# A float32 graph network with Strassen-Winograd products by adj: the first product reads the right half of adj first, and the products that end layers 2 and 3 take adj's tiles as weights

## The chip, the core and the metric

The kernel runs on one core of one Trainium2 chip. The metric is device time in microseconds of one execution, the median over several; lower is better. The profiled execution is a run of its own, whose time is given beside its span.

## What is computed

Four layers on x (8 graphs in a batch, 2048 nodes, 64 features), all with the same 2048 x 2048 matrix adj, all float32. Each layer adds its result to x and normalizes over the features.

```python
# layer 0: A_stack = [I, adj, 2 adj adj - I]; w and b depend on the node
x = layernorm(x + einsum('bnki,nkio->bno', A_stack x, w(embedding)) + b(embedding))
# layer 1: two times z = relu((adj z) W_i)
x = layernorm(x + relu((adj relu((adj x) W_0)) W_1))
# layer 2
x = layernorm(x + x W_self + (adj x) W_neighbor + bias)
# layer 3: x_stack = [x, adj x, 2 adj(adj x) - x] for each of two equal supports
x = layernorm(x + concat(x_stack) W + bias)
```

So there are seven products of adj (2048 x 2048) with a 2048 x 512 matrix (8 graphs x 64 features). The kernel centers weights so that a mean need not be subtracted in most norms, and orders the linear maps so that layer 2 and layer 3 end with a product by adj that is added to something ready: in layer 2, slot 1 of `xy` holds x W_self + bias and slot 0 holds x W_neighbor; in layer 3, slot 1 holds x times its own weights + bias and slot 0 the rest; in both, slot 1 += adj * slot 0, and slot 1 is normalized.

## The kernel before

**Data.** `xy` holds nodes on partitions: 16 tiles of 128 nodes, two slots, 512 columns (4 pairs p of two graphs, 128 columns each). adj comes from memory in two layouts: *slices* for the first product, *blocks* for the six others. Every chunk or block of it is 1 MB and goes through a ring of buffers `a` (four at first; three more, `ring2`, from the second product's end).

**Products by Strassen-Winograd on two levels.** The outer level cuts adj into quadrants A11, A12, A22 and the sums S1 to S4, which makes seven `inner` products; each `inner` does the same once more with eight `mul`s (matrices 0 to 7, of which several are sums). The sums of adj's blocks are made once, during the first product, and kept in DRAM (`comb[q]`); the other six products load them.

**The first product (slices 0 to 3, `plain_slice` and `fast_slice`).** A slice `ns` is a quarter of the target nodes: every fourth tile. It needs four chunks, chunk j holding source nodes of quarter j; chunks 0 and 1 are adj's left half, 2 and 3 its right. The loads are asked for on SP's queue (`slice_chunk`, L149). While TensorE multiplies, VectorE forms the sums (`prepare`, L473): `outer` makes S1 to S4, `inner` makes the second-level sums of each. POOL's queue writes them out (L485, `comb<-si` and `comb<-so`; four buffers `si`, three `so`). Slice 0 is multiplied plainly, chunk by chunk in the order 0, 1, 2, 3 (L618, 128 records of 512 columns). Slices 1 to 3 use the seven outer products (L655) in this order: A11, A12, S1, S2, A22, S3, S4, with T1 to T4, sums of x, against them. `prepare` is a generator and `next(parts)` runs it piece by piece between these products. Results go into `hT` (features on partitions), to DRAM (`t1T`), and by transposes (`back`, L339) into slot 1 of `xy`. `join_bias` adds layer 0's bias to x in the last slice; `sum_weights` and `sum_wn` prepare weights of later layers on VectorE in slices 1 and 2.

**The six other products (`product`).** The order of the outer products is A11, S1, A12, S2, S4, S3, A22. A `mul` is

```python
for m in range(TG):
    nc.tensor.matmul(ps, xb[:, m, :], a[:, :, m, :], ...)   # L228
```

that is, 128 x 128 pieces of x (or a sum of x) are the weights, 512 columns of adj stream past, and the result has features on partitions. A float32 matmul shows as two records in the trace, so a `mul` has eight. VectorE combines the banks (`add`, L201). `onto` adds to what is there: `early` adds the terms that are ready, `finish` the last one, and `hand_over` gives a finished block to the `Pump`, a list of generators that `pump.step` advances once or more per `mul`. The jobs are the features of a layer (`feature1a`, `feature3`, ..., with `project`, L840) and the norms (`layernorm`, L355 to L384).

In the products that end layers 2 and 3 the job is `onto_rest`: it transposes a finished block back to nodes on partitions, four transposes (L889), and adds it to slot 1 (L890). Then the norm follows, and in layer 3 the store.

**Order.** Each engine runs its instructions in the order fixed when the program was built: a scheduler places them by priorities that follow the program's order, and instructions marked `tc.keep_in_program_order` (also called `pin` here) stay in that order among themselves.

Of the kernel before, what the change touches and what calls it, by code (L numbers as in the profile page):

```python
# [9 lines left out]
F32 = mybir.dt.float32  # L10
# [6 lines left out]
P = 128  # L17
# [78 lines left out]
def kernel(  # L96
# [53 lines left out]
        return a  # L150

    chunks = {}
    chunks[0, 0] = slice_chunk(0, 0, TG)
    for t in range(TG):
        nc.scalar.dma_start(xy[:, t, 0, :], x[:, t, :])
    for j in range(1, NG):
        tq = slice(j * TG, (j + 1) * TG)
        nc.sync.dma_start(xy[:, tq, 0, :], x[:, tq, :])
        chunks[0, j] = slice_chunk(0, j)
# [12 lines left out]
    def xcol(slot, t, p):  # L172
        return xy[:, t, slot, ts(p, 2 * F)]


    loads = 0
    banks = 0
# [11 lines left out]
            nc.sync.dma_start(a, comb[q][s].rearrange("p (n m c) -> p n m c", n=TG, m=TG))  # L189
        return a  # L190

    def product(src, feature, between=None, rate=1, own=None, pin=False, batch=1):

# [4 lines left out]
        def add(out, a, b, op=ALU.add):  # L200
            nc.vector.tensor_tensor(out, a, b, op)  # L201
            return out
# [7 lines left out]
        def inner(q, b, finish, early=None):  # L210
# [13 lines left out]

            def mul(ps, s, xb, start, stop=True):
                a = load(q, s)
                for m in range(TG):
                    nc.tensor.matmul(  # L228
                        ps, xb[:, m, :], a[:, :, m, :], start=(start and m == 0),
                        stop=(m == TG - 1), skip_group_check=True,  # L230
                    )
                pump.step(pump.rate)
# [39 lines left out]
        def onto(c, base, give=None, then=None):  # L272

            def early(blk, plus):
                add(c[:, blk, :], base[:, blk, :], plus)

            def finish(blk, ps, plus):
                add(c[:, blk, :], ps, (base if plus is None else c)[:, blk, :])
                if give is not None:
                    hand_over(c, *give, blk)  # L280
                if then is not None:
                    then(blk)
            return finish, early

        def hand_over(c, ih, ch, blk):
            pump.add(feature(2 * ih + blk // 2, 2 * ch + blk % 2, c[:, blk, :]))
# [40 lines left out]

        def last(blk):
            add(v[:, blk], v[:, blk], u[:, blk])
            hand_over(v, 1, 1, blk)  # L330

        inner(S3, t3, *onto(u, u, then=last))
# [75 lines left out]
    if True:  # L408
# [30 lines left out]
            center(wn.rearrange("p n d o -> p (n d) o"), pin=pin)  # L439

        def sum_weights(w3):

            for k in range(2):
                half = slice(k * F, (k + 1) * F)
                nc.vector.tensor_tensor(wd[half, W3A, half], w3[half, 1], w3[half, 3], ALU.add)
                nc.vector.tensor_tensor(w3[half, 2], w3[half, 2], w3[half, 4], ALU.add)
                nc.vector.tensor_tensor(wd[half, W3X, half], w3[half, 0], w3[half, 2], ALU.subtract)
                nc.vector.tensor_scalar(wd[half, W3AA, half], w3[half, 2], 2.0, None, ALU.mult)


            for k in range(2):
                half = slice(k * F, (k + 1) * F)
                center(wd[half, W2N:, half], half)
            for w in (W2S, W3X):
                nc.vector.tensor_tensor(wd[:, w, :], wd[:, w, :], ident, ALU.add)
            for k in range(2):
                half = slice(k * F, (k + 1) * F)
                for n, w in enumerate((W3A, W3X)):
                    nc.vector.tensor_copy(w3o[half, n], wd[half, w, half])
                for n, w in enumerate((W2N, W2S)):  # L460
                    nc.vector.tensor_copy(w2o[half, n], wd[half, w, half])
            center(b2.unsqueeze(1))
            center(b3.unsqueeze(1))

# [1 line left out]
        def prepare(ns, ch, outers):  # L468
# [42 lines left out]
            def put(q, s):  # L511
# [2 lines left out]
                keep(q, 3, flat[:, 3:])  # L514
                inner(q, *(flat[:, k].rearrange("p (m n) -> p m n", m=TG) for k in range(4)))

            outers[S1] = s1 = outer(rq(1, 0), rq(1, 1), ALU.add)
            outers[S2] = s2 = outer(sq(s1), rq(0, 0), ALU.subtract)
            inner(A11, *raw(0, 0))
            outers[S3] = s3 = outer(rq(0, 0), rq(1, 0), ALU.subtract)  # L520
            yield
            put(S1, s1)
            yield
            put(S2, s2)
            outers[S4] = s4 = outer(rq(0, 1), sq(s2), ALU.subtract)
            inner(A12, *raw(0, 1))
            inner(A22, *raw(1, 1))
            yield
            put(S3, s3)
            put(S4, s4)  # L530
# [2 lines left out]
        with tc.tile_pool(name="p_n", bufs=4, space=PSUM) as p_n, tc.tile_pool(  # L533
# [28 lines left out]
            def xq(h, c):  # L562
# [3 lines left out]


            T = [
                xy[:, 2:NT:TG, 1, :].rearrange("p t (h c) -> p t h c", h=2),
                xs.tile([P, NT // 4, 2, 4 * F], F32, tag="T2", name="T2"),  # L570
                xy[:, 3:NT:TG, 1, :].rearrange("p t (h c) -> p t h c", h=2),
                xs.tile([P, NT // 4, 2, 4 * F], F32, tag="T4", name="T4"),
            ]

            def sums_of_x():
# [33 lines left out]
            def plain_slice(ns, ch):  # L609

                ps = [bank() for p in range(NP)]
                for j in range(NG):
                    steps = [(p, m) for p in range(NP) for m in range(TG)]
                    if j == 0:

                        steps = [(p, m) for m in range(TG) for p in range(NP)]
                    for k, (p, m) in enumerate(steps):
                        mm = nc.tensor.matmul(  # L618
                            ps[p],
                            xcol(0, TG * j + m, p),  # L620
                            ch[j][:, m],
                            start=(j == 0 and m == 0),
                            stop=(j == NG - 1 and m == TG - 1),
                            skip_group_check=True,
                        )
                        if j == k == 0:
                            tc.keep_in_program_order(mm)
                hT = [new_h() for p in range(NP)]
                for p in range(NP):
                    nc.scalar.copy(hT[p], ps[p])  # L630
                return hT

            def fast_slice(ns, ch, held):
# [44 lines left out]
                    return u  # L678

                next(parts)  # L680
                pa = mul(bank(), raw(0, 0), x_of(0, 0))
                p1 = sums.tile([P, GW], F32, tag="p1", name="p1")
                nc.scalar.copy(p1, pa)
                load_chunks(ns + 1, 0, 1)
                next(parts)
                p2 = mul(bank(), raw(0, 1), x_of(1, 0))
                if ns == TG - 1:
                    join_bias(0, 1)
                    join_bias(0, 0)
                pc = mul(bank(), summed(S1), t_of(1))  # L690
                for job in held:
                    pump.add(back(*job))
                next(parts)
                if ns == 1:
                    sum_weights(w3)
                elif ns == 2:
                    sum_wn()
                pb_ = mul(bank(), summed(S2), t_of(2))
                u2 = plus("u2", pb_, p1)
                done(0, p2, p1)  # L700
                pd = mul(bank(), raw(1, 1), t_of(4))
                load_chunks(ns + 1, 2, 3)
                nc.vector.tensor_tensor(u2, pc, u2, ALU.add)
                next(parts)
                if ns == TG - 1:
                    join_bias(1, 0)
                mul(pb_, summed(S3), t_of(3), start=False)
                u3 = plus("u3", pb_, p1)
                done(3, pc, u3)
                done(2, pd, u3)  # L710
                pe = mul(bank(), summed(S4), x_of(1, 1))
                done(1, pe, u2)
                return [hT[p] for p in range(NP)]

            for ns in range(TG):
                ch = [chunks.pop((ns, j)) for j in range(NG)]
                if ns == 0:
                    for n, _ in enumerate(prepare(ns, ch, {})):
                        if n == 1:
                            sums_of_x()  # L720
                    hT = plain_slice(ns, ch)
                    w3 = load_weights()
                    load_chunks(1, *range(NG))
                    pump.add(biases())
                else:
                    hT = fast_slice(ns, ch, held)
# [116 lines left out]
                )  # L843
        return z

    def part(g, p, slot):
        return xy[:, g * TG : (g + 1) * TG, slot, ts(p, 2 * F)]


    def feature1a(g, p, hT):  # L850
        nc.scalar.activation(part(g, p, 1), project([(hT, W1A)]), AF.Relu)
# [30 lines left out]
            yield  # L882
        return own

    def onto_rest(g, p, hT):

        pt = p_z.tile([P, TG, P], F32, tag="z", name="pt3")
        for k in range(TG):
            nc.tensor.transpose(pt[:, k, :], hT[:, ts(k, P)], ident)  # L889
        nc.vector.tensor_tensor(part(g, p, 1), pt, part(g, p, 1), ALU.add)  # L890
        yield


    product(1, then(feature1b, 0, mean=True, after=both_terms(0, w2o, b2)), rate=2)
    product(0, then(onto_rest, 1))


    def feature3(g, p, hT):
# [1 line left out]
        yield  # L900

    product(1, feature3, own=both_terms(1, w3o, b3), rate=1.5)
    product(0, then(onto_rest, 1, single=[(1, 0)], store=True), rate=2)
    pump.drain()


# [45 lines left out]
```

## Time and profile before

| what | value |
|---|---|
| median of 3 runs | 1690.9 us (1686.34 to 1692.46) |
| profiled execution, its own time | 1690.62 us |
| its span | 1688.8 us |
| PE busy | 1666.1 us, 5952 records |
| PEld (weight loads) busy | 856.5 us |
| VectorE busy | 942.0 us |
| ScalarE, POOL busy | 265.3 us, 249.6 us |
| mean granted TensorE clock | 0.996 |
| DMA | 391.25 MB, mean 232 GB/s |

The first product lies from about 5.7 to 221 us, layer 0's second product to about 770 us, layer 1's first from there, and so on; the product that ends layer 2 lies from some 1100 to 1300 us, the one that ends layer 3 in the last 200 us. In the timeline a row is a run of like instructions: start, length, engine, line, operation, output and inputs, count, and in brackets the idle time before it with what ended it. Records of matmuls overlap (a 512-column record is 593 ns long, but the next begins after some 429), so the distance of two starts is the time that a matmul takes of TensorE, not its length.

### The profile page before, as it was taken

To read this page: it belongs to the slowest core of one execution; us is meant where nothing else is said; L and a number is where in the kernel's file an instruction comes from. 1 tells how busy PE (TensorE), PEld (TensorE's weight loads), DVE (VectorE), ACT (ScalarE), POOL (GpSimd) and SP (SyncE) were. 2 spreads that over 40 slices of the span, in tenths; PEclk is the share of its full clock that TensorE was granted. 3 is DMA by queue.
4 is the path that set the end of the run, shared out by engine and by line. 5 is a ranking of instruction groups with operands and counts; after the bars stand their busy time and mean duration, and the time that the engine had idled before them with its cause. 6 is when DMAs were issued, how large, how long until landed. Compare 5 with 4: busy or idle time off the path is not lost.

```text
span 1688.8 us, 16180 instructions
## 1 busy us (share of the span) xinstructions
PE 1666.1 (99%) x5952; PEld 856.5 (51%) x5952; DVE 942.0 (56%) x1687; ACT 265.3 (16%) x763; POOL 249.6 (15%) x332
## 2 busy tenths in 40 slices
PE   9899999999999999999999999999999999999997
PEld 4588854444444444444455455554444455554443
DVE  5477884546456656454443365863557444543556
ACT  0000000332323332330011010220001011100001
POOL 1122200443344544450000000000000000000000
PEclk9999999999999999999999999999999999999999
DMA  9898978134333123309877877667888866678883
GB/s 326 328 353 329 331 275 303 62 123 166 109 114 123 52 86 125 112 19 376 303 268 264 310 253 257 226 216 283 291 296 282 306 210 237 231 265 309 316 310 121
DMA packets 82271, 391.25 MB, mean 232 GB/s; under 512 B 8880, under 2 KB 25264, under 8 KB 42640
## 3 DMA queue, kind: packets, MB, share of 16 engines
q1 hardware_dynamic: 69504, 346.78, 58.4%
q0 software_dynamic: 11248, 42.08, 6.5%
q10 hardware_dynamic: 1440, 1.35, 0.2%
q8 instruction: 48, 0.79, 0.2%
q14 instruction: 31, 0.25, 0.0%
HBM read 339.85 MB, written 50.33 MB: 231 GB/s over the span
## 4 chain that ended last, share of the span: by engine, by line
PE 95%; DVE 3%; DMA 1%; POOL 0%; ACT 0%; issue 0%; POOLq 0%; DVEq 0%
PE mmb L228 25%; PE y L792 20%; PE mmc L228 17%; PE mma L228 16%; PE ps_n L655 8%; PE ps_n L618 3%; PE z L840 2%; PE z L872 2%; DMA a<-in_slices 1%; PE pt L831 1%; PE pt L889 1%; DVE ss L371 0%; PE pt_n L339 0%; DVE xy L381 0%; DVE sm L355 0%; DVE xy L356 0%
## 5 line engine op out<-in xcount | busy, mean ns | idle before, releaser
L228 PE MATMUL mmb<-a,t 128*128 128x512 f32 x1008 | 454.9, 593 | 1.1 <-DVE xy L381 1.1
L228 PEld LDWEIGHTS mmb<-a,t 128*128 128x128 f32 x1008 | 188.7, 190 | 229.0 <-issue 224.7
L800 DVE SCALAR_TENSOR_TENSOR xy<-y,e_sb,xy 128x128 f32<-128x128 f32 x512 | 179.7, 351 | 137.5 <-PE y L792 121.6
L809 POOL TENSOR_TENSOR s<-s 128x512 f32<-128x512 f32 (+2 forms) x192 | 159.0, 828 | 339.5 <-ACT s L804 329.3
L804 ACT ACTIVATE s<-y,e_sb 128x128 f32<-128x128 f32 x512 | 138.9, 382 | 270.5 <-PE y L792 270.4
L228 PE MATMUL mma<-a,T 128*128 128x512 f32 x384 | 173.3, 594 | 0.0
L201 DVE TENSOR_TENSOR u<-mmb,p 128x512 f32<-128x512 f32 x84 | 58.0, 690 | 193.8 <-PE mmb L228 188.4
L228 PE MATMUL mmc<-a,t 128*128 128x512 f32 x336 | 151.7, 594 | 0.0
L792 PE MATMUL y<-wn,xT 64*128 64x512 f32 x512 | 133.1, 592 | 0.0
L228 PE MATMUL mma<-a,xy 128*128 128x512 f32 x288 | 130.4, 594 | 2.7 <-DVE C L201 2.6
L792 PE MATMUL y<-wn,tT 64*128 64x512 f32 x512 | 131.3, 589 | 0.0
L792 PE MATMUL y<-wn,C 64*128 64x512 f32 x512 | 131.2, 589 | 0.0
L228 PEld LDWEIGHTS mma<-a,T 128*128 128x128 f32 x384 | 71.4, 190 | 84.3 <-issue 83.5
L201 DVE TENSOR_TENSOR C<-mmc,C 128x512 f32<-128x512 f32 x60 | 41.4, 690 | 101.7 <-PE mmc L228 101.7
L228 PEld LDWEIGHTS mmc<-a,t 128*128 128x128 f32 x336 | 61.9, 190 | 70.9 <-issue 70.4
L228 PEld LDWEIGHTS mma<-a,xy 128*128 128x128 f32 x288 | 53.8, 190 | 68.6 <-issue 62.9
L228 PE MATMUL mmc<-a,T 128*128 128x512 f32 x192 | 86.4, 593 | 0.0
L243 ACT COPY p<-mma 128x512 f32<-128x512 f32 x42 | 24.5, 584 | 377.8 <-PE mma L228 375.8
L792 PEld LDWEIGHTS y<-wn,xT 64*128 64x128 f32 x512 | 49.2, 187 | 63.3 <-issue 62.9
L792 PEld LDWEIGHTS y<-wn,tT 64*128 64x128 f32 x512 | 49.5, 187 | 60.6 <-issue 60.6
L792 PEld LDWEIGHTS y<-wn,C 64*128 64x128 f32 x512 | 49.6, 187 | 60.3 <-issue 60.3
L228 PE MATMUL mmc<-a,xy 128*128 128x512 f32 x144 | 64.9, 593 | 0.0
(114 smaller groups left out, 1587.9 us busy)
## 6 DMA issues: line engine op xcount, KB each, us to landing
a<-comb SPq DMA_DIRECT2D x240, 1024.0 KB, 4.8
a<-in_blocks SPq DMA_DIRECT2D x54, 1024.0 KB, 4.9
comb<-si POOLq DMA_DIRECT2D x28, 1024.0 KB, 10.9
a<-in_slices SPq DMA_DIRECT2D x15, 1024.0 KB, 8.2
comb<-so POOLq DMA_DIRECT2D x16, 512.0 KB, 5.7
comb<-so POOLq DMA_DIRECT2D x16, 256.0 KB, 5.6
t1T<-hT SPq DMA_DIRECT2D x16, 256.0 KB, 4.6
xT<-in_xT SPq DMA_DIRECT2D x16, 256.0 KB, 3.1
```

Source lines behind the costliest of these rows:

```text
L201: nc.vector.tensor_tensor(out, a, b, op)
L228: nc.tensor.matmul(ps, xb[:, m, :], a[:, :, m, :], start=(start and m == 0), stop=(m == TG - 1), skip_group_check=True,)
L243: nc.scalar.copy(p1, pa)
L618: mm = nc.tensor.matmul(ps[p], xcol(0, TG * j + m, p), ch[j][:, m], start=(j == 0 and m == 0), stop=(j == NG - 1 and m == TG - 1), skip_gr ...
L655: nc.tensor.matmul(ps[:, ts(p, GW // 2)], b(k, p), a(k // TG, k % TG), start=(start and p == k == 0), stop=(k == NT // 2 - 1), skip_group_ ...
L792: nc.tensor.matmul(y[:, b, :], terms[n][half, ts(k, P)], wn[half, n, h * DH : (h + 1) * DH, :], start=(n == 0), stop=(n == 2),)
L800: nc.vector.scalar_tensor_tensor(acc, y[:, :, ts(d, F)], e, acc, ALU.mult, ALU.add)
L804: nc.scalar.activation(s[:, d], y[:, :, ts(d, F)], AF.Copy, scale=e)
L809: nc.gpsimd.tensor_tensor(s[:, :n], s[:, :n], s[:, n : 2 * n], ALU.add)
L831: nc.tensor.transpose(pt[:, ts(k, P)], xy[:, g * TG + k, slot, ts(p, 2 * F)], ident)
L840: nc.tensor.matmul(z[:, k, :], aT[:, ts(k, P)], wd[:, w, :], start=(n == 0), stop=(n == len(terms) - 1),)
L872: nc.tensor.matmul(z[n][:, k], xT[half, ts(k, P)], w[half], start=True, stop=True)
```

## The change

Three parts, in one diff.

1. *Right half first.* Slice 0 loads and multiplies its chunks in the order 2, 3, 0, 1 (`AHEAD`). `fast_slice` takes A12 and A22 first, then A11, S1, S2, S4, S3. `prepare` forms A12's and A22's sums first, then S1, S2, S4; A11's and S3's come later. Chunks 2 and 3 of the next slice are asked for after A22, chunks 0 and 1 after S1. T1 and T4 change places. The final sums of a slice are regrouped to fit (`q3`, and `p1` with S1's product added).
2. *adj's tiles as weights.* `product` has a new argument `onto_slot`, used in the products that end layers 2 and 3. With it a `mul` is sixteen matmuls: a 128 x 128 tile of adj is the weight, 128 columns of x (or a sum of x) stream past, and the result has nodes on partitions. `early`, `finish` and `last` add slot 1 of `xy` in and write the result there. `onto_rest` with its transposes and its add is gone; the job `nothing` leads straight to the norm.
3. `sum_weights` and the centering in it are pinned to the program's order.

```diff
+    AHEAD = (2, 3, 0, 1)
+    chunks[0, AHEAD[0]] = slice_chunk(0, AHEAD[0], TG)
+    for t in range(AHEAD[0] * TG, AHEAD[0] * TG + TG):
         nc.scalar.dma_start(xy[:, t, 0, :], x[:, t, :])
-    for j in range(1, NG):
+    for j in AHEAD[1:]:
...
             def mul(ps, s, xb, start, stop=True):
                 a = load(q, s)
+                if onto_slot is not None:
+                    for k in range(TG):
+                        for m in range(TG):
+                            nc.tensor.matmul(
+                                ps[:, ts(k, P)], a[:, k, m, :], xb[:, m, :],
+                                start=(start and k == m == 0), stop=(m == TG - 1), skip_group_check=True,
+                            )
+                    pump.step(pump.rate)
+                    return
...
             def early(blk, plus):
                 add(c[:, blk, :], base[:, blk, :], plus)
+                if give is not None and onto_slot is not None:
+                    add(tiled(c[:, blk, :]), place(*give, blk), tiled(c[:, blk, :]))
 
             def finish(blk, ps, plus):
-                add(c[:, blk, :], ps, (base if plus is None else c)[:, blk, :])
+                if give is not None and onto_slot is not None:
+                    if plus is None:
+                        add(place(*give, blk), place(*give, blk), tiled(base[:, blk, :]))
+                    add(place(*give, blk), tiled(ps), place(*give, blk) if plus is None else tiled(c[:, blk, :]))
+                else:
+                    add(c[:, blk, :], ps, (base if plus is None else c)[:, blk, :])
...
         def last(blk):
             add(v[:, blk], v[:, blk], u[:, blk])
+            if onto_slot is not None:
+                add(place(1, 1, blk), place(1, 1, blk), tiled(v[:, blk]))
             hand_over(v, 1, 1, blk)
...
+            inner(A12, *raw(0, 1))
+            inner(A22, *raw(1, 1))
             outers[S1] = s1 = outer(rq(1, 0), rq(1, 1), ALU.add)
             outers[S2] = s2 = outer(sq(s1), rq(0, 0), ALU.subtract)
-            inner(A11, *raw(0, 0))
-            outers[S3] = s3 = outer(rq(0, 0), rq(1, 0), ALU.subtract)
+            outers[S4] = s4 = outer(rq(0, 1), sq(s2), ALU.subtract)
             yield
             put(S1, s1)
             yield
             put(S2, s2)
-            outers[S4] = s4 = outer(rq(0, 1), sq(s2), ALU.subtract)
-            inner(A12, *raw(0, 1))
-            inner(A22, *raw(1, 1))
+            inner(A11, *raw(0, 0))
+            yield
+            outers[S3] = s3 = outer(rq(0, 0), rq(1, 0), ALU.subtract)
             yield
             put(S3, s3)
             put(S4, s4)
...
                 next(parts)
+                p2 = mul(bank(), raw(0, 1), x_of(1, 0))
+                pd = mul(bank(), raw(1, 1), t_of(4))
+                load_chunks(ns + 1, 2, 3)
+                for job in held:
+                    pump.add(back(*job))
+                next(parts)
                 pa = mul(bank(), raw(0, 0), x_of(0, 0))
                 p1 = sums.tile([P, GW], F32, tag="p1", name="p1")
                 nc.scalar.copy(p1, pa)
+                q3 = plus("u3", pd, p1)
+                done(0, p2, p1)
...
                 pc = mul(bank(), summed(S1), t_of(1))
                 next(parts)
+                load_chunks(ns + 1, 0, 1)
...
                 pb_ = mul(bank(), summed(S2), t_of(2))
                 u2 = plus("u2", pb_, p1)
                 nc.vector.tensor_tensor(u2, pc, u2, ALU.add)
+                nc.vector.tensor_tensor(p1, pc, p1, ALU.add)
                 next(parts)
+                pe = mul(bank(), summed(S4), x_of(1, 1))
+                done(1, pe, u2)
                 if ns == TG - 1:
                     join_bias(1, 0)
                 mul(pb_, summed(S3), t_of(3), start=False)
-                u3 = plus("u3", pb_, p1)
-                done(3, pc, u3)
-                done(2, pd, u3)
-                pe = mul(bank(), summed(S4), x_of(1, 1))
-                done(1, pe, u2)
+                done(3, pb_, p1)
+                done(2, pb_, q3)
...
-    def onto_rest(g, p, hT):
-        pt = p_z.tile([P, TG, P], F32, tag="z", name="pt3")
-        for k in range(TG):
-            nc.tensor.transpose(pt[:, k, :], hT[:, ts(k, P)], ident)
-        nc.vector.tensor_tensor(part(g, p, 1), pt, part(g, p, 1), ALU.add)
-        yield
+    def nothing(g, p, c):
+        yield from ()
...
-    product(0, then(onto_rest, 1))
+    product(0, then(nothing, 1), onto_slot=1)
...
-    product(0, then(onto_rest, 1, single=[(1, 0)], store=True), rate=2)
+    product(0, then(nothing, 1, single=[(1, 0)], store=True), rate=2, onto_slot=1)
```

## The prediction

> **What bounds the kernel now.** I read the page first: engines, then the chain.
>
> ```profile
> PE 1666.1 (99%) x5952; PEld 856.5 (51%) x5952; DVE 942.0 (56%) x1687; ACT 265.3 (16%) x763; POOL 249.6 (15%) x332
> ...
> PE 95%; DVE 3%; DMA 1%; POOL 0%; ACT 0%; issue 0%; POOLq 0%; DVEq 0%
> ```
>
> TensorE is busy for all but 22.7 us, and the chain lies on it. So the change is worth what it does to TensorE's stream, to its few waits, and to the tail behind the last product. PE's waits come next:
>
> ```profile
> PE ps_n L655 <- DMA a<-in_slices: 5.5, 1, 5.5
> PE mma L228 <- DVE C L201: 2.6, 1, 2.6
> PE rise L541 <- POOL ident masks.py:199: 2.1, 1, 2.1
> ```
>
> Only the first lies where the change works (the second is at 403 us, among L792's matmuls). The timeline of PE around it:
>
> ```profile
> 70.23 1.89 PE L655 MATMUL ps_n<-a,xy 128*128 128x256 f32 x8
> 77.59 3.69 PE L655 MATMUL ps_n<-a,xy 128*128 128x256 f32 x8 [5.47 <-DMA a<-in_slices]
> 81.12 0.60 PE L339 MATMUL pt_n<-ident,hT 128*128 128x128 f32 x4
> ```
>
> SP's queue in the timeline, and the table of stages (after the stage's length: PE, PEld, DVE, ACT, POOL busy, then PEclk, DMA share, GB/s):
>
> ```profile
> 60.95 0.33 SPq L149 DMA_DIRECT2D a<-in_slices  x1
> ```
>
> ```profile
> 75.00:80.00 5.00, 2.40 (x6) 1.96 (x7) 3.20 (x6) 0.00 (x0) 0.84 (x2) 0.50 0.13 46
> ```
>
> The fourth chunk of slice 1 can be asked for only when slice 0 has read its fourth chunk (60.95), and lands 16.6 us later; slice 1 wants it at 72.1. After the wait eight records take 3.53 us (77.59 to 81.12) where eight elsewhere take 1.73: the granted clock is 0.50. The stall costs 5.5 + 1.8 = 7.3 us.
>
> Then the stages of layers 2 and 3. One `mul` is eight records (a float32 matmul is two) of 512 columns. Starts in the timeline give true pitches; durations overlap.
>
> ```profile
> 843.02 1.05 PE L840 MATMUL z<-wd,C 128*128 128x128 f32 x8
> 843.91 3.60 PE L228 MATMUL mmc<-a,t 128*128 128x512 f32 x8
> ...
> 1182.60 0.60 PE L889 MATMUL pt<-ident,C 128*128 128x128 f32 x4
> 1183.04 3.60 PE L228 MATMUL mmc<-a,t 128*128 128x512 f32 x8
> ```
>
> ```profile
> 843.02 0.86 PEld L840 LDWEIGHTS z<-wd,C 128*128 128x128 f32 x7 [0.24 <-issue]
> ```
>
> A `mul` alone is 3.434 us (from 1165.43 to 1182.60 there are five). Eight records of 128 columns, each with a fresh 128x128 weight, take 0.89 us; inside such a burst loads follow each other every (0.86 - 0.19)/6 = 0.1117 us. Four transposes take 0.44 (0.437 over several, 109.2 ns each).
>
> **The change part by part.**
>
> *Tiles of adj as weights (two of six products).* 2 x 7 x 8 = 112 calls of `mul` go from 8 records of 512 columns to 32 of 128, the shape of L840's burst: 32 x 111.7 ns = 3.574 us against 3.434, +0.140, x112 = **+15.7 us**. Bounds: below, 109.2 ns, the transposes' pitch (+6.8 us); above, 50.4 us / 384 = 131 ns, L840's busy weight-load time per record (+86 us). I take 111.7: same operands, same shape, and constant from the second record of a burst on.
>
> Here a rule speaks against the change. The Trainium skill, "TensorE: Matmul & The Clock Gate", section "Back-to-back issue gap", says that in a stream of load-and-multiply pairs the weight load sets the pace at small widths: at 128 columns about 81 ns where the formula for the multiply alone gives about 56. Those 25 ns on top of 109.2 would make 134 ns a record, 3584 x 22.5 ns = +81 us over my value, and the change clearly slower. The row shows 2.5 ns on top instead, so I follow the row; that its bursts are only eight long is what stays open.
>
> More PE instructions must also be fetched. The page's DMA queues show it:
>
> ```profile
> q8 instruction: 48, 0.79, 0.2%
> ```
>
> 48 packets for PE's 11904 instructions (one in 250; 66 bytes each), so 112 x 48 = 5376 more are 21 more packets. In the trace's DMA records two of them lie 17.7 us apart (1380.8 and 1398.5 us) with no gap at PE; the new rate is one in 14. Cost nothing; with that cover gone it is part of the third rival.
>
> *The transposes of `onto_rest` go.* 128 in all; 30 groups of four lie in the stream: 30 x 0.437 = **-13.1 us**. The last two are in the tail.
>
> *DVE.* Per product 16 adds of L890 (683 ns) go, and 16 come (three in `early` and one in `finish` for each of three inner products, four in `last`). Nothing on balance. PE waits for DVE where a bank is added to again: the read of `u2`, `u3` has one `mul`, 3.57 us, before the bank is needed. In the new order the worst case I walked (end of S3, start of A22: a final add, a whole layernorm and three adds ahead of `u2`) reads it 7.8 us after S3's end; the bank is wanted at 10.7. Cost nothing, 2.9 us of cover.
>
> *Tail.* Before, the last product stops streaming at 1673.90 + 3.43 = 1677.33, and the span ends 11.5 us later: two blocks' transposes, adds and norms interleave there. From an add (L890 at 1674.27) to the end of its norm (L381, 1677.65 + 0.69) is 4.1 us; from the last L381's end (1685.34) to the span's end 3.5. DVE takes the new chains strictly one after another, each waiting at its final add with nothing else behind it: block 3 starts 0.2 after its product, at -6.9 from the end of the stream, and ends at -2.9; block 2 ends at 1.1, block 1 at 5.2; with 3.5 that is 8.7. **-2.8 us**.
>
> *The first product.* Slice 0 now reads chunks 2, 3, 0, 1; SP's queue holds the same instructions in the same order, with other chunks in them. The last chunk asked for at 60.95 is now (1,1). Ahead of it PE does A12 and A22 (2 x 6.91), the biases (1.93), three transposed groups (1.31) and half of A11's first half (1.73): wanted at 79.5, against 77.6 before. So the stall goes, **-7.3 us**, if nothing delays the chunk. What could: the writes to `comb` on POOL's queue. A12 and A22 of slice 1 (1 MB each) are now computed before that chunk lands; `si` has four buffers, so no more than 4 MB are ever queued, but the queue stays full longer. In the DMA view of 58 to 80 us all engines move some 410 GB/s until 72; 2 MB more are at worst 5.1 us, at best nothing. I take 77.6 + 2.6 = 80.2: **+0.7 us** of wait.
>
> What else is moved. A11's sums and their write go behind S2: in slice 3 written at about 193 instead of 178.85, landed by 205; SP's load of it stands in its queue ahead of two more `a` loads and xT's, and PE wants it at 221. Ten us of cover. S1's sums are wanted at 85 instead of 79, computed 1.2 us after the chunk. `sum_weights`, now pinned behind S3's sums at about 94, is some 5.5 us of DVE; behind it `u2` (S2's product ends at 99) and so PE's S3 at 106: 6 us of cover. The chunks of slices 2 and 3 are asked for no later than before against a start 5 us earlier, and were all there (no wait in the list). T1 and T4 swap their places, nothing else. The bias joins fill DVE waits. One more 0.69 us add per slice lies in such a wait too.
>
> At the end of slice 3 a wait is *added*. Before, the last product was S4 with two short adds behind it, for columns that are transposed last. Now it is S3, with four adds (0.34 apart), and the first transposes' second halves need the third and fourth: 0.2 + 2 x 0.34 + 0.42, then one more 0.34; less the 0.44 of first halves that PE has: **+1.0 us**. DVE's next sums (t2 at about 220.4) come before PE wants them (221).
>
> **Sum:** -7.3 + 0.7 + 1.0 + 15.7 - 13.1 - 2.8 = **-5.8 us** on the profiled execution's own 1690.62 (span 1688.8 and 1.8 around it), 0.3 below the median of 1690.9: **1684.8**. A measurement of this kernel tells about 0.5% (8.5 us) from no change, so this is "within".
>
> **The rivals.**
>
> 1. *The chunk stays late.* The full 5.1 us: landing 82.7, a wait of 3.2 and perhaps part of the 1.8 for the clock: -3.3 to -1.5 us, 1687.3 to 1689.1. For it: DMA is full from 43 to 72. Against: the queue bound of 4 MB.
> 2. *Weight loads hide wholly.* At 109.2 ns per record the products pay 6.8 instead of 15.7: 1675.9, faster. For it: transposes show it. Against: their loads are shorter (141 ns against 190 in the groups).
> 3. *Weight loads become the bound.* In runs of 1800 records without a wide matmul between, the load path falls behind. Place: each product's 56 `mul`s; price 3.6 us per ns; from 113.3 ns a loss, from 115.7 slower by over 0.5%; at 131, 3584 x 19.6 ns = +69 - 5.8, 1755. For it: the page's rule, and PEld is without a gap in the bursts. Against: a burst's pitch does not grow.
> 4. *The form does not change.* The compiled order of the new kernel shows sixteen 128x128 matmuls per `mul` and no L889; nothing left for this.
>
> **How the numbers follow.** Forecast 0.62; rival 1 0.17; rival 2 0.11; rival 3 0.08; 0.02 is for things not seen. The forecast's own spread is some 4 us (0.5 ns of pitch is 1.8, the landing 2, the tail 1), so a third of it falls below 1682.4. Faster: 0.2 + 0.11 + 0.02 = 0.33; slower: 0.08 and the upper end of rival 1, 0.11; within: 0.56. The range takes in rival 1 whole and half of the way to rival 2, and leaves out rival 3: 1677.5 to 1691.5.
>
> **What would show it.** Right: L237's records 111 to 112 ns apart in both products, 3.57 us a `mul`; no PE wait on in_slices over 2 us and PEclk 1.00 at 75 to 80; 1 us of wait on hT near 213; 8 to 9 us from the last product to the end. Wrong: a pitch of 109 or over 113; a wait of several us near 79; new waits of L237 on DVE.

## The result and the profile after

The changed kernel takes 1682.19 us in the median of six runs (1681.9 to 1684.56), the kernel before 1690.7 (1686.34 to 1692.46, six runs beside them). The ratio is 0.9953, with a 95% interval of 0.9939 to 0.9966: 8.5 us less by the medians, 7.9 by the ratio. The prediction said 1684.8, 5.8 us less. The profiled execution is the slowest of the six: 1684.56, span 1682.8.

From the page after, engines, then the chain, then the packets of PE's instruction fetches:

```profile
PE 1666.6 (99%) x8176; PEld 1045.7 (62%) x8176; DVE 946.1 (56%) x1690; ACT 265.9 (16%) x763; POOL 250.3 (15%) x332
...
q8 instruction: 65, 1.06, 0.2%
...
PE 96%; DVE 3%; POOL 0%; ACT 0%; issue 0%; POOLq 0%; DVEq 0%; ACTq 0%
```

TensorE still carries the chain. DMA's 1% in it, the wait for the chunk, is gone. There are 2224 more records, and weight loads rose from 51% to 62% of the span. PE's waits (us in total, times, longest):

```profile
PE mma L244 <- DVE C L207: 2.2, 1, 2.2
PE rise L575 <- POOL ident masks.py:199: 2.1, 1, 2.1
PE pt L868 <- DVE xy L412: 1.5, 2, 1.1
PE mmb L244 <- DVE xy L412: 1.2, 1, 1.2
PE pt_n L370 <- DVE hT L704: 0.7, 1, 0.7
```

No wait on `in_slices` is left; the last row is the new wait at the end of slice 3. The third row has grown: before, its line (L831 there) was

```profile
PE pt L831 <- DVE xy L381: 1.1, 2, 0.7
```

The longer of its two waits, at 1122 us in the product that ends layer 2, is 1.08 us in the changed kernel and in e1 and e8 (part 2 alone), and 0.68 in before and in e2 (without part 2): part 2 adds 0.4 us there.

In the timeline and the table of stages, where before there were 5.47 us of idle time and a clock of 0.50:

```profile
71.40 3.62 PE L689 MATMUL ps_n<-a,xy 128*128 128x256 f32 x16
74.85 0.60 PE L370 MATMUL pt_n<-ident,hT 128*128 128x128 f32 x4
75.29 3.62 PE L689 MATMUL ps_n<-a,xy 128*128 128x256 f32 x16
78.75 0.60 PE L370 MATMUL pt_n<-ident,hT 128*128 128x128 f32 x4
...
82.64 0.60 PE L370 MATMUL pt_n<-ident,hT 128*128 128x128 f32 x4
```

```profile
75.00:80.00 5.00, 5.00 (x29) 4.46 (x27) 0.94 (x1) 1.17 (x2) 0.00 (x0) 1.00 0.58 207
```

The chunk still takes as long to land. It is asked for at 62.12 (SP's queue), and the longest "DMA to landing" of L149 is 16.9 us, so it lands at 79.0. A11's half begins at 79.18 and reads it after eight records (1.73 us), at 80.9: 1.9 us to spare. That is not much: over the seven profiles with this order of products the chunk took from 16.5 to 18.9 us, and in the slowest of them (gap=5 of e9, landing at 80.08) TensorE read it at 80.12, some 0.2 us late.

The new `mul` in the timeline, and the tail:

```profile
1663.40 3.74 PE L237 MATMUL mmc<-t,a 128*128 128x128 f32 x32
...
1666.97 3.74 PE L237 MATMUL mmb<-t,a 128*128 128x128 f32 x32
...
1670.55 3.74 PE L237 MATMUL mmc<-T,a 128*128 128x128 f32 x32
...
1674.62 0.69 DVE L412 TENSOR_TENSOR xy<-xy,rs 128x512 f32<-128x512 f32 x1
1675.23 0.68 DVE L207 TENSOR_TENSOR xy<-mmc,C 128x512 f32<-128x512 f32 x1
...
1678.62 0.69 DVE L412 TENSOR_TENSOR xy<-xy,rs 128x512 f32<-128x512 f32 x1
```

A `mul` every 3.575 us (1670.55 - 1663.40, halved). The last one stops streaming at 1670.55 + 3.57 = 1674.12, and the span ends 8.7 us later; it was 11.5. The last block's norm follows on the norm of the block before it: add at 1675.23, end at 1679.31, then the store.

The time parts cleanly at the products' starts in the traces. Six products follow the first; the fourth of them ends layer 2 and the sixth layer 3, and these two are changed by part 2. The table gives the start of the first of the six (the start of its first `mul`), the start of the fourth, and the time from there to the end of the span, in us:

| kernel, one profile each | wait for the chunk | the six products start | the fourth starts | from there to the end |
|---|---|---|---|---|
| before | 5.5 | 221.69 | 1112.81 | 576.0 |
| before, again (e7) | 5.0 | 222.38 | 1115.13 | 576.0 |
| changed | none | 216.31 | 1108.67 | 574.1 |
| part 2 alone (e1) | 2.0 | 219.04 | 1111.74 | 574.1 |
| part 2 alone, again (e8) | 2.2 | 218.62 | 1109.72 | 574.1 |
| parts 1 and 3 alone (e2) | none | 216.35 | 1106.93 | 576.0 |
| changed, block 2 done first (e3) | none | 216.53 | 1106.71 | 574.1 |
| changed, A11 second (e5) | 6.3 | 224.59 | 1117.78 | 574.1 |
| changed, no pins (e6) | none | 216.71 | 1109.01 | 574.1 |

The last column has two values: part 2 is worth 1.9 us in every profile. The third column is the first product: 216.3 to 216.7 without the wait (215.3 to 215.6 in the profiles of e4 and e9, which are not in the table), 221.7 and 222.4 in before. What moves the middle (1106.71 - 216.53 = 890.2 in one profile, 1108.67 - 216.31 = 892.4 in another) is told at e9.

### The profile page after: what moved, and what is told of

The parts are those of the page before. It is cut to its first block, busy times and chain, and to the rows that moved or that the text cites. A ratio compares the mean times of both kernels' runs of the same rounds, so it can differ in the third digit from the quotient of the medians.

```text
span 1682.8 us, 20633 instructions
## 1 busy us (share of the span) xinstructions
PE 1666.6 (99%) x8176; PEld 1045.7 (62%) x8176; DVE 946.1 (56%) x1690; ACT 265.9 (16%) x763; POOL 250.3 (15%) x332
## 4 chain that ended last, share of the span: by engine, by line
PE 96%; DVE 3%; POOL 0%; ACT 0%; issue 0%; POOLq 0%; DVEq 0%; ACTq 0%
PE y L829 20%; PE mmb L244 17%; PE mmc L244 11%; PE mma L244 11%; PE ps_n L689 9%; PE mmb L237 8%; PE mmc L237 6%; PE mma L237 6%; PE ps_n L652 3%; PE z L877 2%; PE z L906 2%; PE pt L868 1%; DVE ss L402 0%; PE pt_n L370 0%; DVE xy L412 0%; DVE sm L386 0%
## 5 line engine op out<-in xcount | busy, mean ns | idle before, releaser
L244 PE MATMUL mmb<-a,t 128*128 128x512 f32 x672 | 303.6, 593 | 1.2 <-DVE xy L412 1.2
L244 PEld LDWEIGHTS mmb<-a,t 128*128 128x128 f32 x672 | 125.8, 190 | 153.9 <-issue 151.0
L237 PE MATMUL mmb<-t,a 128*128 128x128 f32 x1344 | 157.1, 275 | 0.0
L237 PEld LDWEIGHTS mmb<-t,a 128*128 128x128 f32 x1344 | 153.5, 192 | 0.0
L244 PE MATMUL mma<-a,T 128*128 128x512 f32 x256 | 115.6, 594 | 0.0
L244 PE MATMUL mmc<-a,t 128*128 128x512 f32 x224 | 101.2, 595 | 0.0
L244 PE MATMUL mma<-a,xy 128*128 128x512 f32 x192 | 88.8, 604 | 2.2 <-DVE C L207 2.2
L244 PEld LDWEIGHTS mma<-a,T 128*128 128x128 f32 x256 | 47.6, 190 | 56.9 <-issue 56.5
L244 PEld LDWEIGHTS mmc<-a,t 128*128 128x128 f32 x224 | 41.3, 190 | 47.8 <-issue 47.4
L244 PEld LDWEIGHTS mma<-a,xy 128*128 128x128 f32 x192 | 36.4, 193 | 47.3 <-issue 42.2
```

The source lines that it names most:

```text
L237: nc.tensor.matmul(ps[:, ts(k, P)], a[:, k, m, :], xb[:, m, :], start=(start and k == m == 0), stop=(m == TG - 1), skip_group_check=True,)
L244: nc.tensor.matmul(ps, xb[:, m, :], a[:, :, m, :], start=(start and m == 0), stop=(m == TG - 1), skip_group_check=True,)
```

## The experiments

**e1, part 2 alone.** The first product stays as before.

```
-    product(0, then(onto_rest, 1))
+    product(0, then(nothing, 1), onto_slot=1)
...
-    product(0, then(onto_rest, 1, single=[(1, 0)], store=True), rate=2)
+    product(0, then(nothing, 1, single=[(1, 0)], store=True), rate=2, onto_slot=1)
```

> Only adj's tiles as weights in the two products; the first product as before. An `inner` has seven calls of `mul` (matrices 0, 1, 3 to 7), so 98 calls change, not 112: +98 x 0.140 = +13.7 us; -13.1 for 30 groups of transposes in the stream, -2.8 in the tail: -2.2 us, some 1688.5, with the wait for the fourth chunk and the half clock after it still there (5.6 + 1.8 us near 72 to 81). Rival, the products carry the whole gain (something in them costs less than the rows say): -8 us, 1682.5. Rival, the tiles cost and the first product pays for it: over +2 us.

Measured: 1685.83 us (9 runs), ratio 0.9975 (0.9965 to 0.9985), 4.2 us less: twice what the theory gave. The stages say why. From the fourth product to the end it gained 1.9 us (574.1 against 576.0), about as it should. The rest came from the first product, where nothing was edited (219.04 against 221.69). PE's waits of e1:

```profile
PE ps_n L684 <- DMA a<-in_slices: 2.0, 1, 2.0
```

The chunk, asked for at 61.74 us, landed at 74.96, in 13.2 us instead of 16.6. e7 and e8 ask whether that is chance.

**e2, parts 1 and 3 alone.** The right half first, with the pins; layers 2 and 3 keep `onto_rest`.

```
+    AHEAD = (2, 3, 0, 1)
...
+            inner(A12, *raw(0, 1))
+            inner(A22, *raw(1, 1))
...
-            inner(A11, *raw(0, 0))
...
+            inner(A11, *raw(0, 0))
```

> Only the right half first (with the pinned weights); the last products of layers 2 and 3 with transposes as before. Theory: the wait and the half clock go (-7.4 us) and the wait for hT at the end of slice 3 comes (+0.7): -6.7 us, some 1684; no PE wait on in_slices, PEclk 1.00 from 75 to 80. Rival, the products carry the gain: 0.

Measured: 1685.34 us (7 runs), ratio 0.997 (0.9959 to 0.9981), 5.1 us less (3.2 to 6.9). The wait on `in_slices` is not in its list, the new one of 0.7 us on `hT` is:

```profile
PE pt_n L341 <- DVE hT L675: 0.7, 1, 0.7
```

The rival falls. The expected 6.7 lies at the upper end of the interval, and the stages give 5.7 (216.35 against the mean of 221.69 and 222.38), all of it in the first product. Slice 1 began at 61.96 us here, against 60.76 and 61.40 in before, and the trace accounts for it. TensorE's clock came up from half to full at 7.62 us here and at 5.96 and 7.25 there; 1.66 us more at half clock cost 0.83. And the first matmul of slice 0 began at 6.27 us instead of 5.69, behind a wait for x's tiles:

```profile
PE ps_n L623 <- DMA xy<-in_x: 0.4, 1, 0.4
```

A start 0.58 us later costs half of that, 0.29, since that stretch is at half clock too: 60.76 + 0.83 + 0.29 = 61.88, all but 0.08 us. The wait, 0.3 to 0.4 us long, stands in four of the eight profiles with the right half first (e2, e3, e6, gap=6) and in none of the four with slice 0's old order, so the new order can cost some 0.3 us. Why x's tiles come later was not tried.

**e3, the third block of hT finished before the fourth.**

```
+                done(2, pb_, q3)
                 done(3, pb_, p1)
-                done(2, pb_, q3)
```

> The changed kernel, with the last two sums of a slice exchanged: block 2 (columns that are transposed first) before block 3. Theory: the wait on hT (0.7 us) at the end of slice 3 falls below 0.2: -0.6 us against the changed kernel, which only the wait in the trace can show, not the time. Rival: the transposes of the other columns then wait as long, no change.

Measured: 1682.2 us (5 runs), ratio 0.9951 (0.9938 to 0.9963). No change in time. The wait on VectorE goes from the list, but gaps of 0.25 and 0.51 us between PE's transposes stay at 214.6 and 215.4, and 0.3 of them is now put down to ACT:

```profile
PE pt_n L370 <- ACT xy L371: 0.3, 1, 0.3
```

So the order of the two sums alone does not remove the wait; that the length of the adds and copies behind the slice's last product sets it fits, and no run here changed that length.

**e4, every matmul of `onto_slot` in two halves of 64 columns.** The weights are loaded twice as often, the columns streamed stay the same.

```
-                            nc.tensor.matmul(
-                                ps[:, ts(k, P)], a[:, k, m, :], xb[:, m, :],
+                            for half in range(2):
+                                nc.tensor.matmul(
+                                    ps[:, ts(2 * k + half, F)], a[:, k, m, :], xb[:, m, ts(half, F)],
...
```

> The changed kernel, each matmul of the two products cut in two of 64 columns: 64 records a `mul`, each with its own weight load, the same columns in all. Theory, the weight load sets the 111.7 ns: the pitch stays near 112, a `mul` takes 7.15 us, 98 x 3.57 = +350 us, some 2032. Rival, the columns set it: the pitch falls to about 56 to 64 (the 64-column and the two-row-group records elsewhere stand at 60 to 64 ns), a `mul` takes 3.6 to 4.1 us, at most +52 us.

Measured: 2029.53 us in one run, 347 more than the changed kernel; the theory said 2032, and the rival would have stopped 52 above. The timeline of e4 (the count is of records, two for a matmul):

```profile
1121.11 7.31 PE L238 MATMUL mma<-xy,a 128*128 128x64 f32 x64
1128.26 0.61 PE L238 MATMUL mmb<-t,a 128*128 128x64 f32 x4
```

64 records from 1121.11 to 1128.26 are 111.7 ns each, over the whole trace 111.65 in the mean; with 128 columns, in the changed kernel, it was 111.76. Half the columns cost the same: the pace is that of the weight load, or of something else that each record pays alike, and no run here parts these two. So the third rival had a point, at another price: this form is bound by what each record pays, but at 111.7 ns and not at 115 or more, in long streams as in bursts of eight.

**e5, A11 second instead of third in a slice.** Slice 0, the chunks and SP's queue stay as changed.

```
                 p2 = mul(bank(), raw(0, 1), x_of(1, 0))
+                next(parts)
+                pa = mul(bank(), raw(0, 0), x_of(0, 0))
...
                 pd = mul(bank(), raw(1, 1), t_of(4))
...
-                next(parts)
-                pa = mul(bank(), raw(0, 0), x_of(0, 0))
```

> The changed kernel, with A11 second in each later slice (A12, A11, A22) instead of third; the chunks, their order in SP's queue and slice 0 stay as changed. The chunk asked for last is then wanted one product (6.9 us) earlier, at about 72 us, where it landed at 79. Theory (the gain of the first product comes from wanting that chunk later): a wait of 5 to 7 us on in_slices comes back near 72 us, with or without a few us of half clock behind it; about +5 to +8 us on the changed kernel, 1687 to 1690. Rival (slice 0's order alone, or the new places of T1 and T4, made the gain): no wait over 2 us there, and the time of the changed kernel, 1682.

Measured: 1691.37 us (12 runs), ratio to before 1.0002 (0.9993 to 1.0011): 9.2 us over the changed kernel by the medians, 8.3 by the ratios, and the whole gain is gone. Its timeline:

```profile
71.40 1.89 PE L689 MATMUL ps_n<-a,xy 128*128 128x256 f32 x8
79.59 3.70 PE L689 MATMUL ps_n<-a,xy 128*128 128x256 f32 x8 [6.30 <-DMA a<-in_slices]
83.13 0.60 PE L370 MATMUL pt_n<-ident,hT 128*128 128x128 f32 x4
```

The wait is back at the place where A11's second quarter is read, 6.3 us, and the eight records behind it take 3.54 us instead of 1.73: 6.3 + 1.8 = 8.1. PE's list has one more wait that the changed kernel's has not, at 231.8 us:

```profile
PE mmb L244 <- DVE t L207: 0.6, 1, 0.6
```

With it the sum is 8.7 us, between the two measures. The gain of part 1 is shown to be this: the late chunk is wanted 6.9 us later.

**e6, without the pins in `sum_weights`.**

```
-                pin(nc.vector.tensor_tensor(wd[half, W3A, half], w3[half, 1], w3[half, 3], ALU.add))
+                nc.vector.tensor_tensor(wd[half, W3A, half], w3[half, 1], w3[half, 3], ALU.add)
...
```

> The changed kernel, with the scheduler free again to place the weights' sums (sum_weights without its pins). Theory (they are 5.5 us of VectorE with 6 us of cover): within 1 us of the changed kernel. Rival (the pins keep VectorE free for the sums that TensorE waits for): a new TensorE wait on VectorE between 80 and 125 us, and 2 us or more on the changed kernel.

Measured: 1683.43 us (4 runs), ratio 0.995 (0.9933 to 0.9967): the changed kernel's time within the spread, and no new wait on VectorE. The scheduler moves the sums from about 96 to 102 us to about 88 to 94; TensorE does not notice. Part 3 is worth nothing that can be measured.

**e7, before once more, and e8, part 2 alone once more.** No edit.

> The kernel before, once more, for a second profile of the same program. The profile shown before had a wait of 5.5 us for the chunk; the kernel with only the tiles as weights, whose first product is the same, showed 2.0. Theory (the landing of this chunk moves by some us from execution to execution): a wait between 1 and 6 us that is not 5.5 again, and a half clock behind it or not. Rival (it is a property of the program: part 2 moved it): 5.5 us again, within 0.5. The ratio must be 1.000 within about 0.001, which says what these comparisons can tell.

> Once more the kernel with part 2 alone (adj's tiles as weights in the two products, the first product as before). By the sum with 98 instead of 112 changed calls it should gain 2.2 us (+13.7 - 13.1 - 2.8); it measured 4.2 (2.6 to 5.9). Theory: 2.2 and the rest is spread, so a second measurement lies at 0.998 to 1.000, and the chunk's wait in its profile is as free to be 2 or 5.5 us as in the kernel before. Rival (part 2 shortens the first product's wait too): 0.997 to 0.998 again, and a wait of 2 us again.

Measured: e7 1690.89 us (12 runs), ratio 0.9997 (0.9987 to 1.0007), wait 5.0; e8 1685.63 (13 runs), ratio 0.9975 (0.9963 to 0.9986), wait 2.2. PE's waits of e7, then of e8:

```profile
PE ps_n L655 <- DMA a<-in_slices: 5.0, 1, 5.0
```

```profile
PE ps_n L684 <- DMA a<-in_slices: 2.2, 1, 2.2
```

The same happened twice for each program, and the ratio of part 2 alone came out twice as 0.9975. Chance is unlikely, and the theory of both texts falls: the kernel with part 2 alone gets its chunk after 13.2 and 13.4 us, the kernel before after 16.6 and 16.1. Yet the operations of both kernels on every engine up to there are the same, in the same order. The difference begins in slice 0. VectorE's first sum of the fourth chunk of slice 0, in the timeline of before and of e1:

```profile
30.35 1.22 DVE L473 TENSOR_TENSOR so<-a 128x1024 f32<-128x1024 f32 x1 [1.53 <-DMA a<-in_slices]
```

```profile
28.56 1.23 DVE L502 TENSOR_TENSOR so<-a 128x1024 f32<-128x1024 f32 x1
```

In before it waits for the chunk (2.15 us in e7), in e1 and e8 it doesn't. POOL's writes of `si` and `so` come later, and the last three before slice 1's chunk is asked for go out at 58.57 to 60.38 in before and at 58.77 to 60.58 in e7, but at 55.49 to 57.29 in e1 and at 56.60 to 58.41 in e8. So less may be under way when the chunk is asked for; that this makes it land sooner is argued, not shown. It is the kernel before that stands out: slice 0's last chunk lands at 30.3 and 31.1 us in its two profiles, and between 27.7 and 29.6 in all ten others. Why it lands some 2 us sooner in a program that differs only after 1100 us stays open; where the two programs put their data in memory is one thing that no run here looked at.

**e9, norms deferred by one and two steps more.** The longest wait that the changed kernel still has is at 400 us, where VectorE's norm stands before the sum that TensorE needs.

```
-            product(1, then(feature0, 0, gap=4, pool_sq=True), rate=4, batch=16)
+            product(1, then(feature0, 0, gap=5, pool_sq=True), rate=4, batch=16)
```

> The changed kernel, with layer 1's norms deferred by five steps instead of four (gap=5). The longest wait of TensorE that is left is 2.2 us at 400.5 us, on a VectorE sum that stands behind a norm's L402; that norm waits for a square on POOL, which waits for an ACT scaling (L841) that stood behind the norm before it. Theory (that order on ACT and VectorE sets the wait): a norm one step later lets the scaling go first, the wait at 400 falls under 1 us, and the half clock of 3.4 us behind it with it: 2 to 4 us less, 1678 to 1680. Rival (the last sums of the layer are late by themselves, the norm is drained there in any case): the wait stays between 1.5 and 3 us, the time within 1 us of 1682.

> The same with gap=6. Theory: as with five steps, 1678 to 1680. Rival: the wait at 400 us stays, or a norm now drains later and a wait of the next product on VectorE takes its place; 1681 to 1684.

Measured: gap=5 1680.59 us (1680.43 to 1680.79, 4 runs), ratio to before 0.9942 (0.9923 to 0.9962); gap=6 1680.76 (5 runs), 0.9944 (0.9927 to 0.9962). Both are below the changed kernel's 1682.19, by 1.6 and 1.4 us, a little less than the theory's 2 to 4; the intervals of the ratios overlap with the changed kernel's, so by these runs alone the gain is likely, not settled. All nine runs lie below the lowest of the changed kernel's six (1681.25 against 1681.9), which were taken at another time. The traces are plain. PE's timeline at gap=5 has no wait there:

```profile
397.47 3.60 PE L244 MATMUL mma<-a,xy 128*128 128x512 f32 x8
400.91 3.60 PE L244 MATMUL mmb<-a,t 128*128 128x512 f32 x8
```

The changed kernel's has:

```profile
400.49 5.40 PE L244 MATMUL mma<-a,xy 128*128 128x512 f32 x8 [2.16 <-DVE C L207]
405.72 3.60 PE L244 MATMUL mmb<-a,t 128*128 128x512 f32 x8
```

The same `mul` starts at 400.49 in the changed kernel and then takes 5.23 us instead of 3.44: the granted clock was 0.50 for 3.4 us behind the wait. The table of stages of the changed kernel (PEclk is the third column from the right):

```profile
397.30:400.70 3.40, 1.24 (x4) 0.41 (x3) 2.46 (x6) 0.21 (x1) 0.83 (x1) 1.00 0.93 316
400.70:404.10 3.40, 3.40 (x5) 1.34 (x5) 3.30 (x7) 0.00 (x0) 0.00 (x0) 0.50 0.49 207
404.10:407.50 3.40, 3.40 (x10) 1.49 (x9) 1.19 (x2) 0.59 (x1) 0.00 (x0) 1.00 0.12 14
```

A norm that runs one step later lets ACT's scaling, and so POOL's sums and square, go first, and VectorE no longer stands at L402 with the sum behind it. The wait of 1.2 us on L412 (at 760 us) is gone as well. Part of the gain is given back, by two waits at 546 and 658 us that were not in the changed kernel's list; from PE's waits at gap=5:

```profile
PE y L829 <- DVE xy L837: 1.6, 2, 0.8
```

2.2 + 1.2 - 1.6 = 1.8 us, near the 1.6 of the medians. The theory had counted the half clock in and the two new waits not. The half clock is hardly a part of the medians: the profiled run of the changed kernel, which had it, has a mean granted clock of 0.997, the five others 0.999. Gap=5 and gap=6, 0.2 us apart, are the fastest kernels of all that ran.

## Why the prediction was right, and where it was not

The mechanisms were right and one term was mis-sized. By the steps of the sum:

- *The stall, -7.3, and the residual wait, +0.7.* Shown by e5, which brings the wait back by moving A11, with the `next(parts)` ahead of it; the wait it brings is on the chunk, not on VectorE's sums. The place where the chunk is wanted was right: 18.6 us after the asking by the prediction (79.5 - 60.95), 18.8 as measured (80.9 - 62.12). The landing lay inside its bounds (16.9 us after the asking, between 16.6 and 21.7), so the +0.7 did not occur here; in one of the seven profiles 0.2 of it did. The half clock behind the wait was counted rightly.
- *End of slice 3, +1.0.* 0.7 in the list of waits; in e3, with the two sums exchanged, 0.3 is put down to ACT's copies and the time stays the same. With these three, the first product was to end 5.6 us earlier. It did so by 5.4 in the first pair of profiles, and by 6.0 over all profiles: 222.0 is the mean of the two of before, 216.0 that of the seven without the wait (215.3 to 216.7).
- *adj's tiles as weights, +15.7.* **This is the term that was mis-sized, and by a count, not by the chip.** Its pitch of 111.7 ns was right (111.76). But an `inner` has seven `mul`s and not eight (matrices 0, 5, 1, 6, 4, 3 and 7; there is none for 2, and the "eight `mul`s" in the description of the kernel above and the 2 x 7 x 8 = 112 of the prediction are wrong). It is 2 x 7 x 7 = 98. The changed kernel's page shows it by its PE records: 98 x 24 more and 128 less for the transposes are 2224, the 8176 - 5952 above; 112 would give 2560. The term is 98 x 0.140 = +13.7, and 2.0 us of the missing 2.7 are this. The count was to be had from the page of before, where L228 has 2352 records: six products of 49 `mul`s of eight.
- *Transposes, -13.1, and tail, -2.8.* The tail is 8.7 us, as predicted. With +13.7 part 2 comes to -2.2; the stages have -1.9. The wait of 0.4 us that part 2 adds at 1122 us is as large as the difference.
- *The rule against the change.* The Trainium skill, "TensorE: Matmul & The Clock Gate", section "Back-to-back issue gap", says that in a stream of load-and-multiply pairs both set the spacing, and that the formula for the multiply alone leaves out the load at small widths. e4 agrees in kind: 64 columns run no faster than 128. The extra 25 ns that the prediction's estimate took from its figures would have cost 71 us here with the right count; for these float32 records the extra over the transposes' 109.2 ns is 2.5. The row of the trace was the better guide, and the objection that its bursts were only eight long fell away.
- *Costed at nothing.* Instruction fetches (17 more packets; the 21 of the prediction came of the count of 112) and the pins (e6) show nowhere in TensorE's waits. Two things do: VectorE's work in part 2, by the 0.4 us at 1122, and slice 0's new order, by the wait on `in_x` in half of the profiles (e2), worth some 0.3 us. The prediction had named neither wait.

Added up with the right count and the measured 0.7: -7.3 + 0.7 + 13.7 - 13.1 - 2.8 = -8.8; with the two waits it had at nothing, -8.4 to -8.1, against 8.5 by the medians and 7.9 by the ratio. The profiled executions differ only by 6.1 (1690.62 and 1684.56), because the one after had the half clock at 400 us (1.8 us), which the one before had not, and began slice 1 1.2 us later (61.93 against 60.76), most of it by a clock that came up 2.2 us later at the start (8.15 against 5.96). Of the rivals, the first (late chunk) fell with the list of waits, the second (hidden loads) and the price of the third with the pitch of 111.76 ns; the 69 us in the third's sum should be 70, and its total is right.

The bound of 0.5% between "within" and "faster", 8.5 us, is where the kernel came to lie (0.47% by the ratio, its interval on both sides). With the right count the forecast would have stood at 7.8 us, the prediction's 5.8 and the 2.0, close under it, and the chances of the two should have been near to equal.

## What to carry to other kernels

A wait for a transfer that can't start earlier goes when its consumer moves later: find work of the same stage that needs other data, and check the reach of that move against the landing time (here 6.9 us against waits of 5 to 6.3). Before a row's duration is multiplied by a count from the source, hold the count against the row's own number of records. When a part of a change gains more than its sum says, cut the time at stage boundaries first: the surplus can lie in code that was not touched.

## What the chip showed that was not expected

- *Weights have a floor per record.* Float32 records with fresh 128x128 weights follow each other every 111.7 ns with 128 columns and with 64. Halving the columns of such a matmul gains nothing; with 512 columns to a weight the same work takes 429 ns in the kernel before instead of 4 x 111.76 = 447.
- *A wait's price depends on where it falls.* The same wait of 2.6 us on VectorE near 405 us was followed by full clock in one profile of before and by half clock in the other (eight records in 3.54 and in 4.97 us):

```profile
406.40 3.70 PE L228 MATMUL mma<-a,xy 128*128 128x512 f32 x8 [2.63 <-DVE C L201]
409.94 2.31 PE L228 MATMUL mmb<-a,t 128*128 128x512 f32 x5
```

```profile
407.09 5.14 PE L228 MATMUL mma<-a,xy 128*128 128x512 f32 x8 [2.62 <-DVE C L201]
412.06 2.31 PE L228 MATMUL mmb<-a,t 128*128 128x512 f32 x5
```

  In every trace the stretches of full and half clock between the first change and the last have lengths of whole multiples of 3.41 us (3.4, 6.8, 68.3, 324.3, 392.5, 1669.1), so the clock changes on a grid, which lies elsewhere in each execution. Laid on it, the two waits differ: in the first profile 1.55 us of the 2.63 lie in one window of 3.41 us and 1.08 in the next, in the second 2.15 lie in one window. Over all twelve traces each of the thirteen windows between the first change and the last product's end in which TensorE idled for 2.05 us or more was followed by one of half clock, and none of those with 1.80 us or less was. The bound lies between these two figures, for this kernel and with the matmuls' ends as the profile models them. The Trainium skill, "TensorE: Matmul & The Clock Gate", Part 1, tells of a free-running window of this length and of the half clock after an idle window; here some 60% of a window was enough. One such window costs 1.4 to 1.8 us behind these waits. A stall of 5 to 6 us always fills enough of a window; one of 2.2 to 2.6 us does in some executions, and that adds to the spread of a kernel's runs. How much of the spread it is was not measured; at gap=5, without such a wait, four runs lie within 0.4 us.
- *A transfer's time differed by 3 us between two programs whose code is the same until a millisecond later* (e1 and e8 against before and e7). Why is open. A gain of one part, measured alone, can hold such a shift: the two parts alone gained 4.2 and 5.1 by the ratios, together 7.9. That the sum of the two is more than the whole fits with this: both shortened the same wait.
